# Layer 1 of a two-layer decoder: where the states are added, how the convolution is done, and which banks the scores use

## The chip, the core and the metric

The kernel runs on one core of one Trainium2 chip. A core has five engines that run side by side: TensorE (PE, with its weight loads as PEld) multiplies matrices, VectorE (DVE), ScalarE (ACT) and GpSimd (POOL) work element by element, and SyncE (SP) issues the transfers between memory and the on-chip SBUF. Matmul results land in PSUM, eight banks of 512 f32 per partition. Each engine executes its own instructions in the order in which the program issued them; between engines, semaphores make one wait for another. The metric is the device time of one execution in microseconds.

## The reference

The input is `x`, 64 sequences of 128 tokens with 128 features, with a context of 77 tokens per sequence. Two decoder layers follow one another; each is a mixer, a cross attention with 16 heads over the context, and a feed-forward block, with a residual sum and a layer norm behind each. Layer 0 has a linear attention, a cross attention with an additive bias, and a mixture of ten experts. Layer 1 has a selective scan, a cross attention with a norm of its own, and a feed-forward block with ternary weights. The mixer of layer 1, cut to what matters:

```python
z = x @ W_in + b_in
xc, xr = z[..., :256], silu(z[..., 256:])
xt = causal depthwise convolution of xc over the tokens, 4 taps   # zeros ahead of the first token
xc = silu(xt + conv_b)
dt, Bm, Cm = split(xc @ x_proj_w)                                 # 16 columns each
delta = softplus(dt @ dt_proj_w + dt_bias)
h = exp(delta * A) * h + (delta * xc) * Bm                        # 16 states per channel, step by step over the tokens
y = sum over the 16 states of h * Cm, + xc * D
out = (y * xr) @ W_out + b_out
```

The cross attention of layer 1 computes `softmax(q k / 8) v` with heads of 64; that of layer 0 adds `attn_bias` and a mask to its scores before the softmax.

## The kernel before, in words

Both layers work on groups of four sequences, so that a tile is 128 partitions by 512 columns; there are 16 groups. Layer 0 runs for all groups and leaves its result in memory (`mid`), then layer 1 runs for all groups.

The order of the work is written by a planner, the class `Flow`, when the program is built. Each stage of a group is a generator that yields steps; a step names its engine, a cost in microseconds, its key, the keys that it depends on and the kinds of buffers (slots) that it needs. `Flow.run` keeps up to five groups open and always issues the step that can start first by its own clocks; a group that is further along wins a tie. A buffer can be taken again when the keys in its `until` are done. A ScalarE step that needs another function table ranks 1.3 later. Steps marked `port=True` (those of VectorE and GpSimd that share a way to SBUF) never overlap in the plan. `ahead` moves a step forward in rank. What the planner fixes is the order in which each engine gets its instructions; on the chip the engines wait for data and buffers only.

The mixer of layer 1 in stages:

- `scan_inputs`: loads a group (line 948), transposes it (953, 957), projects it by the first half of `W_in` (`pz`, line 963) into a bank, and ScalarE writes that with the bias into `xp` (line 969), a tile with three zero columns ahead of each sequence. The convolution is four matmuls per half of the channels (line 977), each with a diagonal matrix of one tap (`diag`, line 851) and `xp` shifted by one token. Then silu into `u` (992, 996), the gate from the second half of `W_in` (999, 1008), the projection to dt, B and C (1013) whose rows go to memory (1021), and softplus in pieces (1028 to 1059), the last three of them on GpSimd, ending in `delta` and `du`.
- `spread`: two states make a step. For each step SP fetches the rows of B and of C and spreads them over the partitions, 512 KB each (line 1075), into two buffers each.
- `decays`: ScalarE makes `dA` (line 1090). `states`: VectorE makes `bu = du * B` into PSUM (line 1106) and scans both states (`h`, line 1114). 
- `outputs`: GpSimd multiplies `h` by C in place (line 1138). An order is added by hand: this product starts only after VectorE's `bu` of the next step. TensorE then adds both states into the bank `acc` by matmuls with the identity (line 1151), two matmuls per step, each of which runs as two passes in f32, so four instructions. After eight steps VectorE adds the skip term (1162), and after sixteen come the gate, the output projection (1179), the residual sum (1189) and the norm.

Layer 1's cross attention (`cross_inputs`, `values`, `attend`) makes scores for eight heads at a time (line 1297) in two of five banks, taken one by one: even heads in one, odd heads in the other. VectorE takes the maximum over the context (line 1316, 128x308 elements) and subtracts it (line 1320), once per bank. Exponential, sum, division on GpSimd (1335), transposes (1342), weighted values (1362) and the output projection (1394) follow; the feed-forward block is `feed`.

Layer 0's cross attention (`b_seq`) does the same in two of eight banks (line 586) and adds the bias on VectorE, once per bank (line 603).

Layer 1 has eight PSUM banks: five for general use (`bank`), two for `bu`, one for `acc`.

Of the kernel before, what the change touches and what calls it, by code (L numbers as in the profile page):

```python
# [11 lines left out]
ALU = mybir.AluOpType  # L12
# [25 lines left out]
class Slots(list):  # L38


    def __init__(self, tiles):
        super().__init__(Slot(a) for a in tiles)

# [119 lines left out]
def decoder(ctx: ExitStack, tc: tile.TileContext, t: dict, out: bass.AP):  # L163
# [116 lines left out]
    with (  # L280
# [10 lines left out]
        bank = slots(8, ps, [P, 512], "mm")  # L291
# [215 lines left out]
        def b_load(g):  # L507
# [4 lines left out]
            bias.until = [k + ("sum", b, 1, 1) for b in range(G)]  # L512
# [63 lines left out]
        def b_seq(g, b):  # L576
# [4 lines left out]
            for hf in range(2):  # L581

                def scores(s0, s1, *_):
                    for jj, sc in enumerate((s0, s1)):
                        q4 = slice(32 * (2 * hf + jj), 32 * (2 * hf + jj) + 32)
                        mm(  # L586
                            sc[:, 0 : 4 * M], qT[q4, b * P : (b + 1) * P],
                            kb[q4, b, :, :].rearrange("p h m -> p (h m)"), start=True, stop=True,
                        )

                if hf == 0:
                    *sc, ss, mx = yield PE(0.6, k + ("sc", b, hf), [k + ("qT",), k + ("kb", 3)], scores, bank, bank, sl_s, sl_mx)
# [3 lines left out]
                else:  # L596
                    sc = yield PE(0.6, k + ("sc", b, hf), [], scores, bank, bank)
                for jj in range(2):
                    key = k + ("sum", b, hf, jj)
                    sc[jj].until = key  # L600
                    yield DVE(
                        0.48, key, [k + ("sc", b, hf), k + ("both",)],
                        lambda: dve.tensor_tensor(  # L603
                            s[:, 8 * hf + 4 * jj : 8 * hf + 4 * jj + 4, :],
                            sc[jj].tile[:, 0 : 4 * M].rearrange("p (h m) -> p h m", h=4),
                            bias[:, b, :].unsqueeze(1).to_broadcast([P, 4, M]), ALU.add,
                        ),
                    )
# [228 lines left out]
    with (  # L837
# [10 lines left out]
        diag = new(pc, [P, 2, 4, P], "diag")  # L848
        for c in range(2):
            for k in range(4):  # L850
                dve.tensor_scalar(diag[:, c, k, :], ident, conv_w[:, c, k : k + 1], None, ALU.mult)
# [6 lines left out]
        for c in range(8):  # L858
            bvb = new(p, [P, P], f"xT{c % 2}")
# [15 lines left out]
        pm = new(ps, [P, 3], "mm0")  # L875
# [22 lines left out]
        bank = slots(5, ps, [P, 512], "mm")  # L898
        sl_x = slots(4, p, [P, G, P], "x")
        sl_xT = slots(2, p, [P, W], "xT")  # L900
        sl_xp = slots(2, p, [P, G, P + 3], "xp")
# [33 lines left out]

        for xp in sl_xp:
            pool.memset(xp.tile[:, :, 0:3], 0.0)
# [7 lines left out]
        def scan_inputs(g):  # L945
# [11 lines left out]
            yield ACT(0.6, k + ("xT",), [k + ("pt",)], lambda: nc.scalar.copy(xT.tile, pt.tile))  # L957
            xT.until = k + ("pr", 1)
            pcv = []
            for c in range(2):  # L960
                pz, xp = yield PE(
                    0.95, k + ("pz", c), [k + ("xT",)],
                    lambda z, _: mm(z, W_in[:, c * P : (c + 1) * P], xT.tile, start=True, stop=True), bank, sl_xp,
                )
                pz.until = k + ("xp", c)
                xp.until = k + ("cv", c)
                yield ACT(
                    0.7, k + ("xp", c), [k + ("pz", c)],
                    lambda: act(
                        xp.tile[:, :, 3:], pz.tile.rearrange("p (b s) -> p b s", b=G), AF.Identity,  # L970
                        bias=b_in[:, c : c + 1],
                    ),
                )

                def conv(pv, taps):
                    for i in taps:
                        mm(
                            pv.rearrange("p (b s) -> p b s", b=G), diag[:, c, i, :],
# [655 lines left out]
```

## Time and profile before

| | |
|---|---|
| Time, median of 3 runs | 3838.25 us (3835.81 to 3839.14) |
| The profiled execution's own time | 3840.87 us |
| Its span | 3839.2 us, 55,872 instructions |
| TensorE busy | 3245.0 us (85%) |
| VectorE busy | 2729.6 us (71%) |
| ScalarE busy | 2107.0 us (55%) |
| GpSimd busy | 1448.3 us (38%) |
| GpSimd's products h * C (line 1138) | 256 of 2348 ns |
| TensorE's accumulation (line 1151) | 1024 of 684 ns, busy 565.4 us |
| VectorE's scans (line 1114) | 256 of 2285 ns |
| VectorE's products bu (line 1106) | 256 of 1324 ns |
| Score reductions, subtractions in layer 1 (1316, 1320) | 256 of 465 ns, 256 of 477 ns |
| Score sums in layer 0 (603) | 256 of 468 ns |

The page gives, for one execution, each engine's busy time, the span in forty slices with the busy share of each in tenths, the TensorE clock that was granted in tenths of full speed, and the costliest groups of instructions: line, engine, operation, what is written and read, count, busy time, mean duration, and the idle time of the engine just before them with what ended it. Matmuls overlap one another, so the busy time of a group can be less than count times mean. Answers of the trace add the same for a stretch of the span, the waits (who waited for whom), the chain of work that ended last, and instructions in order of time. Layer 0 ends at about 1508 us in this trace; layer 1's first scan starts at 1571.

### The profile page before, as it was taken

The page shows a single profiled execution, that of the slowest core. Times are in us where ns is not written, and L with a number is a line of the kernel's source. Part 1 is how long each engine was busy: PE and PEld are TensorE (multiplying, and loading weights), DVE is VectorE, ACT ScalarE, POOL GpSimd, SP SyncE. Part 2 cuts the span into 40 slices and gives each one's busy share as a digit, 9 for nine tenths or more (in the row PEclk, how much of TensorE's full clock was granted, in tenths as well). Part 3 has the DMA queues.
Part 4 walks back from the last instruction along what each step waited for, and adds up shares of the span by engine and source line. Part 5 has one row for each costly group of instructions (what it writes and reads, how often), then busy time and mean ns, then how long its engine had stood idle before and what let it go on. Part 6 is the DMA issues. An engine that isn't in the chain of part 4 may idle for free.

```text
span 3839.2 us, 55872 instructions
## 1 busy us (share of the span) xinstructions
PE 3245.0 (85%) x20696; PEld 2080.1 (54%) x20696; DVE 2729.6 (71%) x5399; ACT 2107.0 (55%) x3690; POOL 1448.3 (38%) x1222
## 2 busy tenths in 40 slices
PE   5999999999999998568877978769788978887783
PEld 3676666666666665224643636435544645554462
DVE  5866766666767554577587687786887788778874
ACT  3663555555554422435745757556566657655653
POOL 4321222222222100455345344544445545545531
PEclk8999999999999998789989999879888988988896
DMA  2000000000000001464154151444243435434410
GB/s 84 11 2 22 12 12 12 12 12 12 11 12 12 4 6 53 154 217 168 33 173 152 43 163 62 155 157 126 96 153 125 139 110 169 143 107 140 143 42 6
DMA packets 126134, 312.86 MB, mean 81 GB/s; under 512 B 29714, under 2 KB 51620, under 8 KB 125476
## 3 DMA queue, kind: packets, MB, share of 16 engines
q1 hardware_dynamic: 125860, 309.29, 24.8%
q8 instruction: 162, 2.65, 0.3%
q14 instruction: 112, 0.92, 0.1%
HBM read 299.29 MB, written 9.96 MB: 81 GB/s over the span
## 4 chain that ended last, share of the span: by engine, by line
PE 49%; DVE 21%; POOL 10%; DMA 9%; ACT 5%; issue 4%; SPq 1%; DVEq 0%; POOLq 0%; ACTq 0%
DMA B<-rows 8%; PE mm L770 7%; PE mm L742 7%; PE mm L743 6%; DVE h L1114 5%; POOL h L1138 4%; DVE bu L1106 3%; PE mm L652 3%; PE acc L1151 3%; PE mm L629 3%; PE mm L1342 2%; PE mm L1362 2%; PE mm L586 2%; POOL s L1335 1%; PE mm L1394 1%
## 5 line engine op out<-in xcount | busy, mean ns | idle before, releaser
L1138 POOL TENSOR_TENSOR h<-h,C 128x1024 f32<-128x1024 f32 x256 | 600.6, 2348 | 586.1 <-DVE bu L1106 488.6
L1151 PE MATMUL acc<-h,ident 128*128 128x512 f32 x1024 | 565.4, 684 | 207.1 <-POOL h L1138 184.5
L1114 DVE TENSOR_TENSOR_SCAN h<-dA,bu 128x1024 f32<-128x1024 f32 x256 | 585.1, 2285 | 47.2 <-PE acc L1151 9.7
L1090 ACT ACTIVATE dA<-delta,negA 128x508 f32<-128x508 f32 x512 | 337.7, 711 | 297.5 <-DVE h L1114 292.1
L1106 DVE TENSOR_TENSOR bu<-du,B 128x1024 f32<-128x1024 f32 x256 | 338.9, 1324 | 202.5 <-DMA B<-rows 123.2
L1151 PEld LDWEIGHTS acc<-h,ident 128*128 128x128 f32 x1024 | 199.8, 212 | 473.3 <-POOL h L1138 282.1
L757 ACT ACTIVATE a<-mm 128x512 f32<-128x512 f32 x320 | 187.4, 596 | 328.6 <-PE mm L742 221.1
L770 PEld LDWEIGHTS mm<-w,eh 128*128 128x128 f32 x2560 | 308.6, 193 | 66.1 <-issue 39.4
L742 PE MATMUL mm<-cT,w 128*128 128x512 f32 x640 | 334.8, 605 | 9.5 <-DVE s L603 9.2
L743 PE MATMUL mm<-cT,w 128*128 128x512 f32 x640 | 329.6, 597 | 0.0
L770 PE MATMUL mm<-w,eh 128*128 128x128 f32 x2560 | 315.9, 277 | 11.5 <-DVE eh L760 11.0
L791 DVE SCALAR_TENSOR_TENSOR v<-mm,cw,v 128x128 f32<-128x128 f32 x512 | 143.5, 343 | 217.5 <-PE mm L770 217.2
L760 DVE TENSOR_TENSOR eh<-a,mm 128x512 f32<-128x512 f32 x320 | 214.0, 674 | 58.0 <-ACT a L757 53.5
L612 POOL TENSOR_TENSOR s<-s,mx 128x1232 f32<-128x1232 f32 x64 | 144.3, 2254 | 272.5 <-DVE mx L609 197.9
L1335 POOL TENSOR_TENSOR s<-s,rs 128x1232 f32<-128x1232 f32 x64 | 144.5, 2259 | 217.3 <-DVE rs L1329 183.2
L743 PEld LDWEIGHTS mm<-cT,w 128*128 128x128 f32 x640 | 122.6, 192 | 155.6 <-issue 142.1
L1342 PE MATMUL mm<-ident,s 128*77 128x128 f32 x1024 | 160.3, 310 | 54.9 <-POOL s L1335 46.6
L1297 PEld LDWEIGHTS mm<-kT,qT 64*128 64x128 f32 x2048 | 151.3, 215 | 96.9 <-DVE s L1320 46.5
L1297 PE MATMUL mm<-kT,qT 64*128 64x77 f32 x2048 | 171.5, 309 | 28.3 <-DVE s L1320 27.7
L1342 PEld LDWEIGHTS mm<-ident,s 128*77 128x77 f32 x1024 | 138.4, 171 | 100.9 <-POOL s L1335 64.9
L1353 ACT COPY pT<-mm 77x512 f32<-77x512 f32 x256 | 139.2, 581 | 83.0 <-PE mm L1342 81.1
L1241 PE MATMUL mm<-xT,w_yWq 128*128 128x256 f32 x512 | 161.0, 396 | 15.1 <-ACT kT L1233 9.4
(288 smaller groups left out, 6556.8 us busy)
## 6 DMA issues: line engine op xcount, KB each, us to landing
B<-rows SPq DMA_DIRECT2D x256, 512.0 KB, 4.9
C<-rows SPq DMA_DIRECT2D x256, 512.0 KB, 4.1
cg<-in_ctxT SPq DMA_DIRECT2D x32, 154.0 KB, 2.9
x<-in_x SPq DMA_DIRECT2D x16, 256.0 KB, 3.5
mid<-x SPq DMA_DIRECT2D x16, 256.0 KB, 2.1
xb<-mid SPq DMA_DIRECT2D x16, 256.0 KB, 2.9
x<-mid SPq DMA_DIRECT2D x16, 256.0 KB, 5.4
out<-x SPq DMA_DIRECT2D x16, 256.0 KB, 2.5
```

The lines of the kernel that those rows point to most:

```text
L742: mm(p1, w1[:, e, c * P : (c + 1) * P], xT, start=True, stop=True)
L743: mm(p3, w3[:, e, c * P : (c + 1) * P], xT, start=True, stop=True)
L757: yield ACT(0.6, key + ("silu",), [key], lambda: act(a.tile, p1.tile, AF.Silu), table="silu")
L760: lambda: dve.tensor_tensor(h[:, c, :], a.tile, p3.tile, ALU.mult),
L770: mm(py[:, b * P : (b + 1) * P], hf[:, j % 2, b * P : (b + 1) * P], w2[:, f, j % 2, :], start=j == 0, stop=j == n - 1,)
L1090: act(dA[:, j, :, 1:], delta[:, c, :, 1:], AF.Exp, scale=negA[:, c, n + j : n + j + 1])
L1106: order[g, c, n] = dve.tensor_tensor(bu, du[:, c, :].unsqueeze(1).to_broadcast([P, 2, W]), BC["B", g, c, n], ALU.mult)
L1114: dve.tensor_tensor_scan(h.rearrange("p n s -> p (n s)"), DA[g, c, n].rearrange("p n b s -> p (n b s)"), bu.tile.rearrange("p n s -> p (n ...
L1138: one = pool.tensor_tensor(h, h, BC["C", g, c, n], ALU.mult)
L1151: mm(acc, ident, HS[g, c, n][:, j, :], start=n + j == 0, stop=n + j == NS - 1)
L1297: mm(sc[:, i * M : (i + 1) * M], qT[r, 4 * hf + i, b2 * P : (b2 + 1) * P], kT[r, 4 * hf + i, b2 * M : (b2 + 1) * M], start=True, stop=True,)
L1342: nc.tensor.transpose(pt[0:M, i * P : (i + 1) * P], s[:, 4 * q + i, :], ident)
```

## The change

Three things are changed.

- In layer 1, behind each product `h * C`, GpSimd adds the second state of the step to the first (a new step `pair`, 128x512, marked `port`), and TensorE accumulates one state instead of two: one matmul (two passes) per step. The planner's costs of these steps change with it.
- The convolution's taps are multiplied into the input projection: four weight matrices `taps[k] = W_in[:, 0:256] * conv_w[:, k]` are made once at the start of layer 1, and the convolution is four matmuls from the transposed input itself, whose tile `xT` now has the three zero columns. The projection `pz`, its eviction into `xp` and the `diag` tiles go. The input bias goes into the silu's bias (`conv_all`); at the first three tokens, where taps are missing, a small matmul with three rows (`first` by a piece of the identity, 12 columns) takes the surplus off again. Other readers of `xT` skip the three columns.
- In both layers the scores of a half go into a pair of neighbouring banks, taken together, and VectorE treats both banks in one instruction of 616 elements: in layer 0 the sum with the bias, in layer 1 the maximum and the subtraction. The banks are numbered as four pairs in layer 0, and as two pairs and a single one in layer 1; single users take any half.

```diff
+class Both:
+    def __init__(self, tile_, parts):
+        self.tile, self.parts = tile_, parts
+    @property
+    def until(self):
+        u = [p.until for p in self.parts]
+        if None in u:
+            return None
+        return [key for v in u for key in (v if isinstance(v, list) else [v])]
...
+def banks(pairs, singles):
+    one, two = Slots([]), Slots([])
+    one.extend(Slot(s) for s in singles)
+    for pair in pairs:
+        halves = [Slot(pair[:, i, :]) for i in range(2)]
+        one.extend(halves)
+        two.append(Both(pair, halves))
+    return one, two
...
-        bank = slots(8, ps, [P, 512], "mm")
+        bank, bank2 = banks([new(ps, [P, 2, 512], f"mm{i}") for i in range(4)], [])
...
-                for jj in range(2):
-                    key = k + ("sum", b, hf, jj)
-                    sc[jj].until = key
-                    yield DVE(
-                        0.48, key, [k + ("sc", b, hf), k + ("both",)],
...
+                sc.until = k + ("sum", b, hf)
+                yield DVE(
+                    0.8, k + ("sum", b, hf), [k + ("sc", b, hf), k + ("both",)],
...
-        diag = new(pc, [P, 2, 4, P], "diag")
-        for c in range(2):
-            for k in range(4):
-                dve.tensor_scalar(diag[:, c, k, :], ident, conv_w[:, c, k : k + 1], None, ALU.mult)
+        taps = new(pc, [P, 4, 256], "taps")
+        nc.sync.dma_start(out=taps.rearrange("p k c -> p (k c)"), in_=t["conv_rows"].to_broadcast([P, 1024]))
+        dve.tensor_tensor(taps, taps, W_in[:, 0:256].unsqueeze(1).to_broadcast([P, 4, 256]), ALU.mult)
+        conv_all = new(pc, [P, 2], "conv_all")
+        dve.tensor_reduce(conv_all, conv_w, AX.X, ALU.add)
+        dve.tensor_tensor(conv_all, conv_all, b_in[:, 0:2], ALU.mult)
+        dve.tensor_tensor(conv_all, conv_all, conv_b, ALU.add)
+        first = new(pc, [3, 256], "first")
+        b_first = new(p, [3, 256], "B1")
+        nc.sync.dma_start(out=b_first, in_=rows("b_row", 256, 3))
+        missing = new(p, [3, 3, 256], "B0")
+        pool.memset(missing, 0.0)
+        for k in range(3):
+            nc.sync.dma_start(
+                out=missing[0 : 3 - k, k, :],
+                in_=t["conv_rows"][:, k * 256 : (k + 1) * 256].to_broadcast([3 - k, 256]),
+            )
+        dve.tensor_tensor(first, missing[:, 0, :], missing[:, 1, :], ALU.add)
+        dve.tensor_tensor(first, first, missing[:, 2, :], ALU.add)
+        dve.scalar_tensor_tensor(first, first, -1.0, b_first, ALU.mult, ALU.mult)
...
-        bank = slots(5, ps, [P, 512], "mm")
+        bank, bank2 = banks([new(ps, [P, 2, 512], f"mm{i}") for i in range(2)], [new(ps, [P, 512], "mm2")])
...
-        sl_xT = slots(2, p, [P, W], "xT")
-        sl_xp = slots(2, p, [P, G, P + 3], "xp")
+        sl_xT = slots(2, p, [P, G, P + 3], "xT")
...
-                pz, xp = yield PE(
-                    0.95, k + ("pz", c), [k + ("xT",)],
-                    lambda z, _: mm(z, W_in[:, c * P : (c + 1) * P], xT.tile, start=True, stop=True), bank, sl_xp,
-                )
...
+                def conv(pv, ks):
+                    pv = pv.rearrange("p (b s) -> p b s", b=G)
+                    cs = slice(c * P, (c + 1) * P)
+                    for i in ks:
+                        mm(pv, taps[:, i, cs], xT.tile[:, :, i : i + P], start=i == 0, stop=False)
+                    if 3 in ks:
+                        edge = ident[0:3, 0:3].unsqueeze(1).to_broadcast([3, G, 3])
+                        mm(pv[:, :, 0:3], first[:, cs], edge, start=False, stop=True)
...
-                yield POOL(2.0, ("C", g, c, n), deps, product, ahead=AHEAD, port=True)
+                yield POOL(2.2, ("C", g, c, n), deps, product, ahead=AHEAD, port=True)
+                pair = HS[g, c, n]
+                yield POOL(
+                    1.3, ("pair", g, c, n), [], lambda: pool.tensor_tensor(pair[:, 0], pair[:, 0], pair[:, 1], ALU.add),
+                    ahead=AHEAD, port=True,
+                )
 
                 def add(acc):
-                    for j in range(2):
-                        mm(acc, ident, HS[g, c, n][:, j, :], start=n + j == 0, stop=n + j == NS - 1)
+                    mm(acc, ident, pair[:, 0, :], start=n == 0, stop=n + 2 == NS)
...
-                    *sc, s, mx = yield PE(1.2, k + ("sc", b, hf), [kk + ("k", 7)], scores, bank, bank, sl_s, sl_mx)
+                    sc, s, mx = yield PE(1.2, k + ("sc", b, hf), [kk + ("k", 7)], scores, bank2, sl_s, sl_mx)
...
-                for o in range(2):
-                    sc[o].until = k + ("sub", b, hf, o)
-                    h4 = slice(8 * hf + 4 * o, 8 * hf + 4 * o + 4)
-                    sc4 = sc[o].tile[:, 0 : 4 * M].rearrange("p (i m) -> p i m", i=4)
-                    yield DVE(
-                        0.45, k + ("max", b, hf, o), [k + ("sc", b, hf)],
...
+                sc.until = k + ("sub", b, hf)
+                h8 = slice(8 * hf, 8 * hf + 8)
+                sc8 = sc.tile[:, :, 0 : 4 * M].rearrange("p o (i m) -> p o i m", i=4)
...
+                yield DVE(
+                    0.8, k + ("max", b, hf), [k + ("sc", b, hf)],
+                    lambda: dve.tensor_reduce(by_half(mx.tile), sc8, AX.X, ALU.max),
+                )
```

## The prediction

> **What bounds the kernel now.** I read the slices first, then the busy time by stage, then the waits of the engine that stays fullest, then the shapes that the change touches. The slices split the run in two.
>
> ```profile
> PE   5999999999999998568877978769788978887783
> ...
> DVE  5866766666767554577587687786887788778874
> ...
> POOL 4321222222222100455345344544445545545531
> PEclk8999999999999998789989999879888988988896
> ```
>
> The stages, as stretch, length, then busy time (instructions) of PE, PEld, DVE, ACT, POOL, granted clock, DMA share, GB/s (from two answers):
>
> ```profile
> 0.00:1508.00 1508.00, 1423.06 (x10630) 965.78 (x10630) 997.40 (x2679) 755.88 (x1314) 368.15 (x513) 0.98 0.05 15
> ...
> 2776.00:3575.00 799.00, 665.39 (x3740) 418.25 (x3740) 644.44 (x1009) 505.55 (x889) 403.69 (x264) 0.88 0.41 134
> 3679.00:3839.00 160.00, 92.68 (x748) 69.80 (x747) 84.22 (x252) 74.67 (x148) 36.73 (x46) 0.76 0.02 6
> ...
> 1571.00:3839.00 2268.00, 1781.69 (x9964) 1095.90 (x9964) 1717.78 (x2683) 1322.30 (x2339) 1072.88 (x701) 0.88 0.38 125
> ```
>
> Layer 0 (to 1508) is TensorE's: 94% busy at clock 0.98. Layer 1 (from 1571) is nobody's alone: PE 79%, DVE 76%, ACT 58%, POOL 47%. In the regular part, 2776 to 3575, six groups take 799 us, 133 each, and PE (83%) and DVE (81%) share the lead. So work taken from PE is worth only what DVE waits for PE. Those waits, DVE's own, for the whole of layer 1:
>
> ```profile
> engine line waited for: us in total, times, longest us
> DVE bu L1106 <- DMA B<-rows: 123.2, 113, 4.0
> DVE bu L1106 <- POOL du L1059: 76.3, 12, 8.4
> DVE xb L1401 <- PE mm L1394: 73.3, 18, 10.5
> DVE mx L1316 <- PE mm L1297: 49.1, 35, 7.0
> ...
> DVE x L1534 <- PE mm L1528: 24.0, 12, 2.9
> ```
>
> With three smaller ones (9.7 and 5.3 on acc, 1.4 on L1179) DVE loses 163 us to PE, 76 to POOL and 123 to the landing of B. The shapes:
>
> ```profile
> L1138 POOL TENSOR_TENSOR h<-h,C 128x1024 f32<-128x1024 f32 x256 | 600.6, 2348 | 586.1 <-DVE bu L1106 488.6
> L1151 PE MATMUL acc<-h,ident 128*128 128x512 f32 x1024 | 565.4, 684 | 207.1 <-POOL h L1138 184.5
> ...
> L1106 DVE TENSOR_TENSOR bu<-du,B 128x1024 f32<-128x1024 f32 x256 | 338.9, 1324 | 202.5 <-DMA B<-rows 123.2
> ```
>
> Last, what happens when GpSimd and DVE both read two SBUF operands: the timeline at the start of group 12 (start, length), where a GpSimd add of the size that the change adds begins 0.07 us ahead of DVE's bu product.
>
> ```profile
> 3174.94 1.27 POOL L1217 TENSOR_TENSOR xb<-x,bo_all 128x512 f32<-128x512 f32 x1
> 3175.01 2.29 DVE L1106 TENSOR_TENSOR bu<-du,B 128x1024 f32<-128x1024 f32 x1 [7.46 <-POOL du L1059]
> ```
>
> The bu product takes 2.29 us there and 1.23 alone (its median in the line's own view): it waits for the add to end, then runs. The scan, which reads only one operand from SBUF, keeps its 2.29 us beside any GpSimd product.
>
> **The change part by part.** The sum is made against the profiled execution, 3840.87 us with a span of 3839.2; the median of the timed runs, 3838.25, is 2.6 below it.
>
> Accumulation. 512 of 1024 acc matmul passes go: half of 565.4, -283 us of PE. The first half of the input projection goes too, -36.8 (its 64 passes, line 963), and 64 tiny edge passes come; the nearest rows are the 128-column f32 passes at 0.28 us (line 770), so at most +18. PE in layer 1: 1782 - 283 - 37 + 18 = 1480 us, 65% instead of 79%. By queueing, waits go as load over idle share: 0.79/0.21 = 3.8 to 0.65/0.35 = 1.9, a half of 163, so -82. But the clock speaks against the whole half: the rows give 0.98 at 94% busy, 0.88 at 83%, 0.76 at 58%. A line through the last two gives 0.79 at 65%, with which 1480 us become 1650 (73%, ratio 2.7, waits -47). I take -60, between the two; the ends are 0 and -163.
>
> The page "TensorE: Matmul & The Clock Gate" of the Trainium skill (Part 1) has a harder rule: only half and full clock exist, and an idle window of about 3.4 us drops to half. If the freed PE time fell in such windows, PE would give DVE nothing back, and the sum would be 60 us worse; the 0.88 that a PE busy 79% was granted speaks for the mixture instead.
>
> The pair add. GpSimd gets 256 adds of 128x512. The rows with two tensors of that shape (lines 1411, 1217, 1172, 1417) have means from 1.27 to 1.49, and 1.27 where nothing disturbs; half of the 2.35 product is 1.17. I take 1.27: 325 us, POOL from 1073 to 1398 of 2268 (62%). It still fits, so the add itself costs nothing as long as the next product waits for bu anyway (488.6 us of such idle time now). Two things behind it do cost. First, turns: the product of step i starts when bu of step i+1 ends and takes 2.35, the scan beside it 2.29, so in a run of steps the new add starts just when bu of step i+2 wants to. Over the 224 steps that have a step two behind them in their group, bu starts within 1.27 us after the product's end in about 73; the overlap adds up to 90 us. Ends: 0 (the planner holds the two apart by its shared-port clock and puts reductions between) and 90. I take 30, a third: steps in a run already wait for B (123 us), and part of the delay falls into that. Second, du: the three GpSimd steps before a group's first bu queue behind products, and now adds; one add each in the 12 groups that wait now, 12 x 1.27 = +15 (ends 0 and 41, two adds in 16 groups). The accumulator's matmuls start 1.27 later and take half as long; three h buffers cover it, since a step comes every 6.6 us in the regular part and holds h for about 8; without that cover the scan would wait, as it does for 9.7 us now. B and C are freed by bu and the product, not by the add, so SP's queue is moved only where the product is late, which the 30 hold.
>
> On the same edit the Trainium skill's page "GPSIMD Engine Reference" (sections 4.1 and 8) advises VectorE for elementwise work and names contention with DVE instructions that have two SBUF inputs. Read as every bu paying, it would make the term 325 us, and the change 248 us slower by my other terms; the trace shows the mechanism but also that most bu start when GpSimd is between products.
>
> Convolution. Without pz and its eviction (line 969, 21.9 us of ACT) a group's inputs lose some 2 us of latency. That is worth nothing while the first conv matmul waits for the u buffer, which the output projection two groups earlier frees: for group 12 conv begins at 3032, as that projection ends, while pz began at 2943. Without that cover, 14 groups x 2 = -28. Setup: the eight diag products (1.66) go; a 512 KB broadcast, four small loads and seven short DVE operations come, and five issues of about 0.4 us go ahead of the weights and of the first x on SP's queue. Bounds -3 and +7 (B's landing 4.9 plus the issues 2.0); I take +2. The strided copy into xT has its like in line 969, 0.69 against 0.58, on an ACT that is 58% busy: 0.
>
> Scores in bank pairs. From reductions of 308 and 1232 elements, 465 and 1426 ns, an element costs 1.04 ns, so 616 take 785 instead of 2 x 465, a saving of 145; the subtraction 797 instead of 2 x 477, saving 157. 128 of each: -39 us on DVE, which sits in the lead, so I count all of it (other end 0). Layer 0's sum saves 148 x 128 = 19 us on a DVE that is 66% busy under a PE at 94%: 0. The price: a score needs one of two given pairs rather than any two of five banks, and the trace has no such wait. Its nearest row is PE's wait for score banks (line 1297 on DVE's subtraction), 27.7 us, and 46.5 on the weight loads; ends -20 (both banks come free earlier, at 1.6 us instead of 1.9) and +75. I take +5, near the PE row's lower part, since PE has more air.
>
> Sum: -60 + 30 + 15 + 0 + 2 - 39 + 5 = -47. 3840.9 - 47 = 3794, and less 2.6 for the median: **3791**.
>
> **The rivals.** (1) Much faster: PE and DVE bound the period by turns, and with PE at 92 us of a group's 133 instead of 111 the period follows the fullest engine at the 83% that it has now: DVE's 107, less 2.4 of scores, so 105 / 0.83 = 126, 7 us less over 15 groups, -105: 3733. For it: 480 of the 1791 us of the chain of waits between 1700 and 3500 are PE's. Against it: in the regular part DVE waits mostly for du and B, not for PE. (2) Nothing lands: savings of 99 against other terms of 99, 3838. (3) Slower by turns: in runs of back-to-back steps every bu pays 1.27 for the add in front. Without the turns my sum is -77, so it decides from 77 / 1.27 = 61 steps that pay in full; if a freer PE lets the planner pack scans denser and 120 of 256 pay, that is 152 - 77 = +75: 3913. For it: 67 of the steps now follow within 3.7 us; against it: they wait for B two steps on. (4) Score pairs starve: a single user takes one half of each pair and the scores of the 64 sequences each come 1.2 us late, +75 for the 5 I took: 3861. Against it: five banks are rarely full.
>
> **How the numbers follow.** A measurement here can tell about 0.2% (8 us). Forecast (3755 to 3830) 0.41; rival 1 0.21; rival 2 0.08; rival 3 0.20; rival 4 0.10. Faster 0.62, same 0.08, slower 0.30. The unknown terms alone would reach from 3585 (all good ends) to 4051 (all bad ones); 3690 to 3900 leaves out about a fifth: the lower end of rival 1 and the upper half of rival 3. The likeliest case's own range is 3755 to 3830.
>
> **What would show it.** Acc matmuls 512, busy near 290 to 330; GpSimd adds at 1.27; score reductions 128 at 0.79. bu's mean above 1.32 and DVE's idle time on PE down from 163 toward 100 are my two main terms. Layer 1's granted clock between 0.80 and 0.88. Layer 0's end within 10 us of 1508. I am wrong if bu's mean passes 1.6, if PE waits for DVE at the score matmuls by over 100 us, or if layer 0 moves.

## The result, and the profile after

The changed kernel takes 4219.01 us (median of 4 runs, 4213.41 to 4222.31) against 3838.69 us for the kernel before in the same comparison: ratio 1.0988, 95% interval 1.0969 to 1.1007. It is 380 us slower, and the forecast of 3791 us (range 3690 to 3900) was wrong in sign and by more than the range.

The stages of the changed kernel, in the columns of the stage rows of the prediction (stretch, length, busy time of PE, PEld, DVE, ACT, POOL, clock, DMA share, GB/s):

```profile
0.00:1762.00 1762.00, 1520.08 (x10630) 975.47 (x10630) 1000.45 (x2551) 749.52 (x1304) 368.15 (x513) 0.96 0.05 13
1825.00:4216.00 2391.00, 1713.30 (x9456) 1067.72 (x9456) 1790.14 (x2427) 1288.56 (x2298) 1476.72 (x958) 0.78 0.36 118
```

Two thirds of the loss lie in layer 0, the stage to which the prediction gave nothing: it ends at 1762 instead of 1508 (+254 us). TensorE executes the same 10,630 instructions there, but is busy 86% of the time instead of 94%. Layer 1 takes 2391 us instead of 2268 (+123). From the end of layer 0 to the first scan, with the setup of the taps, it takes 65 us, against 63 before.

The groups that the change touches, from the page after (busy time, mean ns, then the idle time ahead of them and what ended most of it):

```profile
L1178 POOL TENSOR_TENSOR h<-h,C 128x1024 f32<-128x1024 f32 x256 | 607.7, 2374 | 336.0 <-issue 93.4
...
L1195 PE MATMUL acc<-h,ident 128*128 128x512 f32 x512 | 387.3, 850 | 303.8 <-POOL h L1190 276.8
...
L1146 DVE TENSOR_TENSOR bu<-du,B 128x1024 f32<-128x1024 f32 x256 | 398.0, 1555 | 102.2 <-DMA B<-rows 96.2
...
L1190 POOL TENSOR_TENSOR h<-h 128x512 f32<-128x512 f32 x256 | 384.8, 1503 | 19.5
```

Half of the accumulating passes are gone, but a pass takes 850 ns instead of 684. The `bu` products pay 231 ns each more (1324 to 1555), and the new add takes 1503 ns.

VectorE's waits in layer 1 (who waited for whom: total us, times, longest):

```profile
DVE bu L1146 <- DMA B<-rows: 96.2, 66, 8.4
DVE mx L1366 <- PE mm L1347: 88.9, 42, 13.3
DVE fh L1542 <- ACT fh L1538: 56.5, 27, 7.1
DVE h L1154 <- PE acc L1195: 46.2, 28, 6.2
DVE xb L1452 <- PE mm L1445: 36.3, 16, 5.0
```

The wait of `bu` for `du`, 76.3 us before, is nearly gone (3.6); but the maximum over the scores waits longer for TensorE (88.9 against 49.1), and so does the scan for the accumulation (46.2 against 9.7). TensorE does less in layer 1, and VectorE waits for it more: 252 us in all its waits for TensorE there, against 163 before.

### The profile page after: what moved, and what is told of

Its sections match the earlier page's. It is cut to its first block, busy times and chain, and to the rows that moved or that the text cites. A ratio compares the mean times of both kernels' runs of the same rounds, so it can differ in the third digit from the quotient of the medians.

```text
span 4216.8 us, 54152 instructions
## 1 busy us (share of the span) xinstructions
PE 3272.0 (78%) x20184; PEld 2061.2 (49%) x20184; DVE 2805.7 (67%) x5014; ACT 2061.2 (49%) x3632; POOL 1852.6 (44%) x1479
## 4 chain that ended last, share of the span: by engine, by line
PE 46%; DVE 25%; ACT 10%; POOL 8%; DMA 5%; issue 4%; SPq 1%; DVEq 0%; ACTq 0%; POOLq 0%
PE mm L798 6%; DVE h L1154 5%; PE mm L770 5%; PE mm L771 5%; DMA B<-rows 4%; DVE bu L1146 4%; POOL h L1178 3%; PE mm L680 2%; PE mm L1413 2%; PE mm L1393 2%; PE acc L1195 2%; PE mm L657 2%; PE mm L1445 2%; PE mm L1315 2%; PE mm L1347 2%
## 5 line engine op out<-in xcount | busy, mean ns | idle before, releaser
L1154 DVE TENSOR_TENSOR_SCAN h<-dA,bu 128x1024 f32<-128x1024 f32 x256 | 585.5, 2287 | 76.4 <-PE acc L1195 46.2
L1195 PE MATMUL acc<-h,ident 128*128 128x512 f32 x512 | 387.3, 850 | 303.8 <-POOL h L1190 276.8
L1146 DVE TENSOR_TENSOR bu<-du,B 128x1024 f32<-128x1024 f32 x256 | 398.0, 1555 | 102.2 <-DMA B<-rows 96.2
L1190 POOL TENSOR_TENSOR h<-h 128x512 f32<-128x512 f32 x256 | 384.8, 1503 | 19.5
L770 PE MATMUL mm<-cT,w 128*128 128x512 f32 x640 | 348.0, 626 | 44.1 <-DVE v L819 15.4
L798 PE MATMUL mm<-w,eh 128*128 128x128 f32 x2560 | 333.7, 283 | 44.5 <-DVE eh L788 30.5
L771 PE MATMUL mm<-cT,w 128*128 128x512 f32 x640 | 337.7, 610 | 5.2 <-DVE v L819 3.6
L1195 PEld LDWEIGHTS acc<-h,ident 128*128 128x128 f32 x512 | 105.1, 245 | 454.9 <-POOL h L1190 391.4
L1393 PE MATMUL mm<-ident,s 128*77 128x128 f32 x1024 | 181.3, 331 | 82.8 <-POOL s L1386 43.3
L1347 PE MATMUL mm<-kT,qT 64*128 64x77 f32 x2048 | 179.5, 330 | 61.0 <-DVE s L1370 33.5
L1347 PEld LDWEIGHTS mm<-kT,qT 64*128 64x128 f32 x2048 | 160.4, 237 | 134.4 <-DVE s L1370 57.3
L1393 PEld LDWEIGHTS mm<-ident,s 128*77 128x77 f32 x1024 | 150.6, 184 | 139.6 <-POOL s L1386 69.9
L1288 PE MATMUL mm<-xT,w_yWq 128*128 128x256 f32 x512 | 176.6, 428 | 45.8 <-ACT kT L1280 25.6
```

Of the source, the lines that this page charges most:

```text
L770: mm(p1, w1[:, e, c * P : (c + 1) * P], xT, start=True, stop=True)
L771: mm(p3, w3[:, e, c * P : (c + 1) * P], xT, start=True, stop=True)
L798: mm(py[:, b * P : (b + 1) * P], hf[:, j % 2, b * P : (b + 1) * P], w2[:, f, j % 2, :], start=j == 0, stop=j == n - 1,)
L1146: order[g, c, n] = dve.tensor_tensor(bu, du[:, c, :].unsqueeze(1).to_broadcast([P, 2, W]), BC["B", g, c, n], ALU.mult)
L1154: dve.tensor_tensor_scan(h.rearrange("p n s -> p (n s)"), DA[g, c, n].rearrange("p n b s -> p (n b s)"), bu.tile.rearrange("p n s -> p (n ...
L1190: 1.3, ("pair", g, c, n), [], lambda: pool.tensor_tensor(pair[:, 0], pair[:, 0], pair[:, 1], ALU.add),
```

## The experiments: what the bank pairs cost

From this profile I suspected neither the add nor the shortage of banks. Every bank that a single user takes is now a half of a tile of two banks. When the program is built, its dependencies follow tiles, so a matmul that writes one half could be made to wait for the readers of the other half, with which it has nothing to do. The rivals: GpSimd's add (its turns with VectorE), and the taking of scores in pairs.

**Halves without pairs, layer 0.** No score is taken in a pair here; each half is a bank of its own in the plan.

```diff
-        bank = slots(8, ps, [P, 512], "mm")
+        pairs = [new(ps, [P, 2, 512], f"mm{i}") for i in range(4)]
+        bank = Slots([pair[:, i, :] for pair in pairs for i in range(2)])
```

> The kernel before, with layer 0's eight banks made as the halves of four two-bank tiles; every engine keeps its instructions and their order. Theory S (shared tiles: a matmul into one half of a tile waits for the reader of the other half): layer 0 ends near 1700 to 1760 us instead of 1508, and the time is 4030 to 4090. Theory O (order: scores come late because two given banks must be free together, and the planner builds a worse order): the order is the old one, so 3838 within 10.

Measured: 4118.75 us, ratio 1.0747 (1.0716 to 1.0778), some 29 us above the range that the shared tile was given, and far from its rival's. The two programs, laid side by side as built, have the same instructions in the same order on every engine, in the same eight banks. They differ in the waits alone: 621 of TensorE's instructions, some 400 of ScalarE's and 350 of VectorE's wait for a later event or for one more engine. Nearly all of TensorE's changed waits (618 of 625) are for an instruction that uses the other half of the same tile. The trace shows the same stretch of TensorE's work in both kernels (start, length, line, and in brackets the idle time ahead with what ended it). Before:

```profile
668.53 0.38 PE L667 MATMUL mm<-w_xWo,oT 128*128 128x128 f32 x2
668.75 0.81 PE L398 MATMUL mm<-w_w_qkv,T 128*128 128x384 f32 x2
669.40 1.02 PE L742 MATMUL mm<-cT,w 128*128 128x512 f32 x2
...
673.54 1.91 PE L629 MATMUL mm<-ident,s 128*77 128x128 f32 x16
675.29 0.81 PE L398 MATMUL mm<-w_w_qkv,T 128*128 128x384 f32 x2
```

With halves:

```profile
781.94 0.38 PE L668 MATMUL mm<-w_xWo,oT 128*128 128x128 f32 x2
782.16 0.81 PE L399 MATMUL mm<-w_w_qkv,T 128*128 128x384 f32 x2
783.93 1.13 PE L743 MATMUL mm<-cT,w 128*128 128x512 f32 x2 [0.96 <-DVE eh L761]
...
788.43 1.91 PE L630 MATMUL mm<-ident,s 128*77 128x128 f32 x16
791.20 0.88 PE L399 MATMUL mm<-w_w_qkv,T 128*128 128x384 f32 x2 [0.86 <-ACT pT L621]
```

The same matmuls take 6.76 us from the first to the last start before, and 9.26 us here: an expert's projection (line 743) first waits for VectorE's `eh` of an earlier one, and later the projection of line 399 waits for ScalarE's copy of `pT`. These waits are short and many, so the list of waits hardly shows them. The idle time between TensorE's expert matmuls (line 770 before, 771 here) tells more, first before, then with halves:

```profile
L770 PE MATMUL mm<-w,eh 128*128 128x128 f32 x2560 | 315.9, 277 | 11.5 <-DVE eh L760 11.0
```

```profile
L771 PE MATMUL mm<-w,eh 128*128 128x128 f32 x2560 | 330.7, 281 | 54.9 <-DVE eh L761 41.4 <-ACT kb L553 3.6 <-DVE y L466 3.3
```

**The same in layer 1**, with four of its five banks as halves.

```diff
...
-        bank = slots(5, ps, [P, 512], "mm")
+        pairs = [new(ps, [P, 2, 512], f"mm{i}") for i in range(2)]
+        bank = Slots([new(ps, [P, 512], "mm2")] + [pair[:, i, :] for pair in pairs for i in range(2)])
```

> The kernel before, with four of layer 1's five banks made as the halves of two two-bank tiles; order unchanged. Theory S: layer 1 grows by 60 to 130 us, the time is 3900 to 3970. Theory O, and theory T (GpSimd's adds and VectorE's bu products take turns, and that is layer 1's loss): 3838 within 10.

Measured: 4000.59 us, ratio 1.0427 (1.0405 to 1.0448), again above the range of the theory that it bears out. The order is that of before, and some 440 of TensorE's instructions have a later or an additional wait, all of them for an instruction that uses the other half of the same tile. So shared tiles alone cost 166 us in layer 1, although TensorE is busy only 79% of the time there.

**The change with layer 0's scores and banks as before.**

```diff
-        bank, bank2 = banks([new(ps, [P, 2, 512], f"mm{i}") for i in range(4)], [])
+        bank = slots(8, ps, [P, 512], "mm")
...
-                    (sc,) = yield PE(0.6, k + ("sc", b, hf), [], scores, bank2)
+                    sc = yield PE(0.6, k + ("sc", b, hf), [], scores, bank, bank)
...
```

> The changed kernel with layer 0's scores and banks put back. Layer 0 should end at 1508 again and layer 1 keep its 123 us: 3965, between 3950 and 3980.

Measured: 3972.13 us (median of 2 runs), ratio 1.0358 (1.033 to 1.0386), inside the range. Layer 0 ends at 1510. So layer 0's pairs are worth 0.063 of the time, 242 us of the 380.

**The change with single banks in both layers**; the add and the convolution remain. Layer 0's edits are those just shown, layer 1's are of the same kind.

```diff
...
-        bank, bank2 = banks([new(ps, [P, 2, 512], f"mm{i}") for i in range(2)], [new(ps, [P, 512], "mm2")])
+        bank = slots(5, ps, [P, 512], "mm")
...
```

> The changed kernel with the scores of both layers put back to two single banks each, so that the GpSimd add and the new convolution stay. Theory S for the whole loss: the prediction's remaining terms, -60 + 30 + 15 + 2 = -13, so 3826, between 3780 and 3850. Theory T: layer 0 is healed and layer 1 keeps its 123 us, so 3960.

Measured: 3883.11 us, ratio 1.0125 (1.0102 to 1.0147), between the values of the two theories (3826 and 3960). Layer 1's pairs thus cost 0.023, some 89 us net: less than the 166 us of the halves alone. The merged reductions are the likely difference, but the order of the work differs too. And without any pair the kernel is still slower than before: the rest of the sum was wrong as well.

**Pairs that nobody shares, layer 0.** The kernel before, with layer 0's scores in one pair of banks of their own, merged sums, and six single banks for everything else.

```diff
-        bank = slots(8, ps, [P, 512], "mm")
+        bank = slots(6, ps, [P, 512], "mm")
+        bank2 = Slots([new(ps, [P, 2, 512], "sc0")])
...
```

> The kernel before with layer 0's scores in one pair of banks of their own, one VectorE instruction per pair, and the other six banks single tiles. Theory S: nobody shares a tile, so layer 0 ends within 20 us of 1508 and the time is 3825 to 3860 (two banks fewer for the rest). Theory O (a pair is scarce): with a single pair it is scarcer than in the changed kernel, so layer 0 grows by more than 100 us.

Measured: 3868.5 us, ratio 1.0092 (1.0069 to 1.0115), with layer 0's end at 1548. That is above both bounds of theory S (3860, and 20 us from 1508), and far from the 100 us and more of theory O. Merged scores with nothing shared cost about 40 us in that layer, not 250: the pair as such, two banks fewer for the rest, and the new order together are a small part of it. A gain of the merged sums isn't to be seen in this stage, whose bound is TensorE. The same was not tried in layer 1.

## The experiments: what the add costs, and what the relief brings

**The add alone**, on the kernel before, with the planner's costs of the change.

```diff
-                yield POOL(2.0, ("C", g, c, n), deps, product, ahead=AHEAD, port=True)
+                yield POOL(2.2, ("C", g, c, n), deps, product, ahead=AHEAD, port=True)
+                pair = HS[g, c, n]
+                yield POOL(
+                    1.3, ("pair", g, c, n), [], lambda: pool.tensor_tensor(pair[:, 0], pair[:, 0], pair[:, 1], ALU.add),
+                    ahead=AHEAD, port=True,
+                )
...
-                    for j in range(2):
-                        mm(acc, ident, HS[g, c, n][:, j, :], start=n + j == 0, stop=n + j == NS - 1)
+                    mm(acc, ident, pair[:, 0, :], start=n == 0, stop=n + 2 == NS)
...
-                    (acc,) = yield PE(1.9, ("acc", g, c, n), [("C", g, c, n)], add, sl_acc)
+                    (acc,) = yield PE(0.86, ("acc", g, c, n), [("pair", g, c, n)], add, sl_acc)
...
```

> The kernel before with the GpSimd add of a step's two states alone. Theory S: -55 + 30 + 15 = -10, so 3828, between 3790 and 3860. Theory T: 3930 to 3960, with bu's mean at 1.5 us or more and the adds' mean above 1.4.

Measured: 3878.66 us, ratio 1.0108 (1.0081 to 1.0135): slower by a good 1%, and between the two theories. `bu` has a mean of 1594 ns and the add one of 1535.

**Relief without the add.** TensorE accumulates only the first state, and GpSimd adds nothing.

```diff
-                    for j in range(2):
-                        mm(acc, ident, HS[g, c, n][:, j, :], start=n + j == 0, stop=n + j == NS - 1)
+                    mm(acc, ident, HS[g, c, n][:, 0, :], start=n == 0, stop=n + 2 == NS)
...
-                    (acc,) = yield PE(1.9, ("acc", g, c, n), [("C", g, c, n)], add, sl_acc)
+                    (acc,) = yield PE(0.86, ("acc", g, c, n), [("C", g, c, n)], add, sl_acc)
...
```

> The kernel before, with TensorE accumulating only the first state of each step and no add on GpSimd (the second state's part of the sum is left out). It has the relief of TensorE without the adds. If the relief is worth what the prediction took for it, 55 to 60 us, this is 3780; the single add's run stands at +44, so the adds would then cost about 100, in line with the 127 us by which VectorE's own instructions grew there. If TensorE's relief is worth nothing because VectorE is the fuller engine, 3830 to 3845, and the adds cost about 45.

Measured: 3912.88 us, ratio 1.0209 (1.0186 to 1.0232): with 512 passes fewer the kernel is slower, which none of the values foresaw. Two suspects were left: the planner's cost of 0.86, which moves the order of everything in layer 1, and the clock, which falls in that layer from 0.88 to 0.79. The next two kernels tell them apart.

**The same relief in the order of before**: half_acc with the planner's cost left at 1.9.

```diff
-                    (acc,) = yield PE(0.86, ("acc", g, c, n), [("C", g, c, n)], add, sl_acc)
+                    (acc,) = yield PE(1.9, ("acc", g, c, n), [("C", g, c, n)], add, sl_acc)
...
```

> The kernel before, except that TensorE accumulates only the first state of a step (what the second state gives to the output is left out; GpSimd adds nothing), and unlike in half_acc the planner's cost of that step stays 1.9, so that every engine keeps the order of before. 512 of the 1,024 accumulating passes go, some 280 us of TensorE's busy time at the clock of before. Theory R (order): half_acc was slower because the changed cost made the planner order all of layer 1 anew; with the old order the relief shows: 3,780 to 3,825 us, ratio 0.985 to 0.997. Theory K (clock): the freed time lowers the granted clock (0.79 in half_acc against 0.88) and the remaining matmuls use it up, whatever the order: 3,834 us and above, with layer 1's clock below 0.83 and passes of 0.8 us.

Measured: 3805.18 us, ratio 0.9916 (0.9896 to 0.9936), inside the range of theory R. The clock of layer 1 falls to 0.81 and the remaining passes take 800 ns, as theory K had it, and yet the kernel gains:

```profile
L1150 PE MATMUL acc<-h,ident 128*128 128x512 f32 x512 | 360.4, 800 | 260.9 <-POOL h L1138 239.0 <-DVE u L1161 20.8 <-DVE s L1319 1.1
```

**The order alone**: the kernel before, all its work in place, with only the planner's cost at 0.86.

```diff
-                    (acc,) = yield PE(1.9, ("acc", g, c, n), [("C", g, c, n)], add, sl_acc)
+                    (acc,) = yield PE(0.86, ("acc", g, c, n), [("C", g, c, n)], add, sl_acc)
...
```

> The kernel before with the same work, where only the planner's cost of an accumulating step is 0.86 instead of 1.9, as the change has it. Theory R (order): the new order of layer 1 alone costs some 2 per cent, 3,880 to 3,930 us, ratio 1.012 to 1.025, with TensorE's share and its clock in layer 1 as before or a little below. Theory K (clock): the order is worth little, 3,820 to 3,850 us, ratio 0.997 to 1.004.

Measured: 3926.32 us, ratio 1.0234 (1.0212 to 1.0255), as R has it. A number that no instruction carries costs 91 us.

**The add in the order of before**: issued in the product's own step, costs 2.0 and 1.9 as before.

```diff
                         tc.add_manual_dep(one.ins, order[behind].ins.name, BEHIND, reason="shared reads")
+                    pool.tensor_tensor(h[:, 0], h[:, 0], h[:, 1], ALU.add)
...
-                    for j in range(2):
-                        mm(acc, ident, HS[g, c, n][:, j, :], start=n + j == 0, stop=n + j == NS - 1)
+                    mm(acc, ident, HS[g, c, n][:, 0, :], start=n == 0, stop=n + 2 == NS)
```

> The kernel before with GpSimd's add of the two states issued straight behind the product in the product's own step, and the planner's costs of before (2.0 for GpSimd's step, 1.9 for TensorE's), so that the order of every engine is that of before. Against half_same it has the add alone on top. Theory T (turns): VectorE's time grows by 100 to 130 us as in add_only (bu at 1.55 to 1.65 us) and the step of GpSimd by 1.5 us; ratio 0.02 to 0.04 above that of half_same. Theory R (order): most of the 1.1 per cent of add_only came from the planner's new order, so this kernel lies at 0.99 to 1.003, and only some 40 us above half_same.

Measured: 3913.87 us, ratio 1.0197 (1.0175 to 1.0219). Against the same kernel without the add (3805.18) it is 109 us, 0.028 of the time before: theory T, except that VectorE grows a little less than it said. R is wrong here: in this order the add has a cost of its own. With the planner's new costs, and the add as a step of its own, the same work takes 35 us less (3878.66 against 3913.87). The price holds for the order of before alone: with the cost 0.86 the kernel with the add (1.0108) is faster than the one without (1.0209), but the planner orders those two differently. The stages of layer 1 carry it; first the relief alone, then relief and add:

```profile
1571.00:3806.00 2235.00, 1637.75 (x9452) 1028.41 (x9452) 1720.89 (x2683) 1323.13 (x2341) 1072.00 (x702) 0.81 0.38 127
```

```profile
1571.00:3919.00 2348.00, 1655.07 (x9452) 1033.04 (x9452) 1815.06 (x2685) 1328.38 (x2346) 1473.38 (x959) 0.81 0.36 121
```

VectorE's busy time grows by 94 us of the 109 (1720.89 to 1815.06), though its instructions are the same. GpSimd is at 63%, so it is not full. The groups of `bu` and of the add in the second kernel, and `bu` in the first:

```profile
L1106 DVE TENSOR_TENSOR bu<-du,B 128x1024 f32<-128x1024 f32 x256 | 421.9, 1648 | 183.0 <-DMA B<-rows 106.2 <-POOL du L1059 74.2 <-DVE xb L1401 0.2
L1143 POOL TENSOR_TENSOR h<-h 128x512 f32<-128x512 f32 x256 | 380.9, 1488 | 20.1
```

```profile
L1106 DVE TENSOR_TENSOR bu<-du,B 128x1024 f32<-128x1024 f32 x256 | 341.0, 1332 | 187.6 <-DMA B<-rows 107.7 <-POOL du L1059 75.6 <-DVE xb L1400 0.2
```

`bu` takes 81 us more. How, the timeline of the kernel with the add shows (start, length):

```profile
2990.41 1.27 POOL L1143 TENSOR_TENSOR h<-h 128x512 f32<-128x512 f32 x1
2990.93 1.84 DVE L1106 TENSOR_TENSOR bu<-du,B 128x1024 f32<-128x1024 f32 x1 [1.45 <-DMA B<-rows]
...
3004.24 2.35 POOL L1138 TENSOR_TENSOR h<-h,C 128x1024 f32<-128x1024 f32 x1
...
3005.60 2.09 DVE L1106 TENSOR_TENSOR bu<-du,B 128x1024 f32<-128x1024 f32 x1 [0.56 <-DMA B<-rows]
...
3006.67 2.13 POOL L1143 TENSOR_TENSOR h<-h 128x512 f32<-128x512 f32 x1
```

A `bu` that starts 0.52 us into an add waits 0.75 us for its end and is done 1.09 us after that. The second `bu` starts during a product and is done 1.10 us after its end, and the add that starts while this `bu` runs is stretched in turn (2.13). Over the whole run, 92 of the 256 `bu` start while GpSimd is idle and take 1.23 us in the mean; 113 start during an add and take 1.88, which makes 73 us; 35 start during a product and take 1.82, which makes 21 us, against 8 without the add. The wait does not go into the wait for B, as I had hoped: `bu` waits 106.2 us for B with the add and 107.7 without, and pays its turn on top.

**The planner's cost at the measured duration.** Since a wrong number cost 91 us, would the right one gain? A step of two passes takes about 1.4 us.

```diff
-                    (acc,) = yield PE(1.9, ("acc", g, c, n), [("C", g, c, n)], add, sl_acc)
+                    (acc,) = yield PE(1.4, ("acc", g, c, n), [("C", g, c, n)], add, sl_acc)
...
```

> The kernel before with the same work, where the planner's cost of an accumulating step is 1.4, its measured duration (two passes of 0.684 us), instead of 1.9. Theory R as 'an honest cost gives a better order': at or below before, 3,800 to 3,838 us, ratio 0.990 to 1.001. Theory R as 'any other order than the one of before costs': 3,850 to 3,930 us, ratio 1.004 to 1.024.

Measured: 3855.24 us, ratio 1.0057 (1.0036 to 1.0078). This is in the range of the second reading, that any other order costs. The honest cost is not the best one; 1.9 gives the better order of the three that were run. Why that order is better stays open. The same 500 us of layer 1, for the kernel before, half_same, cost_only and add_same in this order:

```profile
2900.00:3400.00 500.00, 420.52 (x2343) 263.19 (x2342) 401.68 (x613) 323.04 (x576) 254.88 (x166) 0.89 0.42 140
```

```profile
2900.00:3400.00 500.00, 391.53 (x2315) 253.28 (x2310) 421.50 (x656) 325.92 (x574) 254.47 (x163) 0.86 0.41 138
```

```profile
2900.00:3400.00 500.00, 382.49 (x1909) 222.60 (x1907) 373.44 (x527) 274.45 (x486) 238.71 (x148) 0.86 0.40 133
```

```profile
2900.00:3400.00 500.00, 386.81 (x2303) 248.96 (x2302) 413.01 (x641) 313.90 (x553) 343.73 (x222) 0.86 0.39 131
```

In the new order (third) every engine does less in the same stretch: no engine is the bound, all of them wait more.

**The convolution alone**, on the kernel before: taps in the projection, everything else as it was.

```diff
-                        mm(
-                            pv.rearrange("p (b s) -> p b s", b=G), diag[:, c, i, :],
-                            xp.tile[:, :, i : i + P], start=i == 0, stop=i == 3,
-                        )
...
+                        mm(pv, taps[:, i, cs], xT.tile[:, :, i : i + P], start=i == 0, stop=False)
...
```

> The kernel before with the taps multiplied into the input projection alone. The prediction's terms: +2 for the setup, 0 to -30 for the latency, and a few us for TensorE's 37 less: 3825 to 3842. If the conv stands on the path of a group's inputs: 3800 to 3815.

Measured: 3851.62 us, ratio 1.0048 (1.0034 to 1.0062), some 18 us slower and above both expectations. TensorE's and ScalarE's work fell as planned: 64 passes of the projection go (36.8 us), 64 small ones come (12.4 us busy), and so do ScalarE's 32 evictions (21.9 us). But steps that go change the plan, as a cost does: VectorE's scaling `fh<-fh,q` (128x512, one source in SBUF) goes from 502 to 759 ns, 16.5 us in all, and the accumulating passes from 684 to 708. Whether that is the whole cause wasn't told apart from the order as such. Next to the add (1.0125 against 1.0108) the convolution can't be told from nothing.

Of the kernels that do all of the work none is faster than the one before.

## Why the prediction was wrong

In units of the time before, the change of +0.099 is made of 0.063 for layer 0's pairs, 0.023 for layer 1's, about 0.002 (not told from nothing) for the convolution, and 0.011 for the add with its relief. These are differences of kernels whose planned orders differ too, so each holds that as well. Step by step:

- **"Scores in bank pairs ... I take +5"** is the step that decided. It asked how often a pair is free, looked for the price at PE's wait for score banks, and so found ends of -20 and +75. The price was in the `banks` function: every single user got half of a shared tile, and with it false dependencies. Halves alone cost 284 us in layer 0 and 166 in layer 1. That layer 0 counted 0 in the sum was the same error: a stage with TensorE at 94% has no air for later waits, of which the run with the halves had 621. Rival 4 had the right place, and its condition named the halves of a pair, but it priced 75 us at 64 sequences in layer 1. Of the three signs of being wrong only "if layer 0 moves" came true: `bu`'s mean stayed below 1.6 (1.555), and at the score matmuls TensorE waits for VectorE only 33.5 us in layer 1 (for the subtraction) and 17.9 in layer 0 (for the sum). The halves runs, in which no score is paired, show that the price falls on every user of the banks.
- **"-39 us on DVE"**, the merged score instructions: the sizes were right, 784 and 791 ns measured (785 and 797 forecast). The gain is not visible beside what sharing costs.
- **Turns, "I take 30, a third", and du, +15**: the mechanism was right, the size was not. In the order of before the add costs 109 us against 45 for both terms, inside the sum of their ends (0 to 131). `bu` pays 81 us. More of them start within an add than the 73 that I had counted (113), and each loses 0.65 us. So the end of 90 was the better value, and the third that I took of it was a hope: the delay did not fall into the wait for B. VectorE's one-source scaling `fh<-fh,q` takes turns too (494 to 659 ns, 10.6 us), which I had not counted. The du term is nothing: 75.6 us of waits without the add, 74.2 with it.
- **"I take 1.27" for the add** holds where nothing disturbs; the mean is 1488 to 1535 ns, since GpSimd also waits for its turn.
- **"I take -60" for TensorE's relief**: it brings 31 us in the order of before, inside its ends, but not by the road described. TensorE's busy time in layer 1 falls from 1782 to 1638 us where 283 us of passes go, as the clock falls from 0.88 to 0.81: the forecast of 1650 at 0.79, which had the convolution's 19 us less in it, was close for this kernel, while the changed kernel has 1713 at 0.78. The clock records of these traces hold 0.5 and 1.0 alone, so that 0.88 is a mean over time; the relief is neither nothing, as the prediction had it for freed time that all falls into half clock, nor 60. VectorE's waits for TensorE hardly move (`xb` 73.3 to 75.2, `mx` 49.1 to 48.9). What falls is `bu`'s wait for B (123.2 to 107.7) and small ones. The rule that waits go as load over idle share has no support here.
- **The planner's costs** were no term of the sum at all. They are part of the diff, and in the runs they are worth from -35 us (with the add, which is a step of its own there) to +108 us (half_acc against half_same), as much as any of the engines' terms.
- **The convolution, 0,** was +18 us alone, outside its ends of -28 to 0, and nothing measurable beside the add. The setup, +2, can't be told: from the end of layer 0 to the first scan it is 63 us before, 65 in the changed kernel, 62 in the one without any pairs and 60 in the one with the convolution alone.

Of the rivals, (3), slower by turns, had the mechanism of a good part of what is left without the pairs (1.0125, 3883 us against its 3913). That the times are close is partly luck, since the relief was smaller than its sum had it and the planner's costs were not in it. On this row the Trainium skill's page "GPSIMD Engine Reference" (section 8), which warns of contention with VectorE where an instruction has two SBUF inputs or uses a two-port mode, agrees with the runs in kind for `bu` (1332 to 1648 ns). The skill's page "VectorE: DVE Perf Modes" (section "Mode 2×_2P — use both read ports for one tensor") would explain the one-source scaling (494 to 659 ns): by that section such an operation may read its tensor through both ports. No run here shows the mode itself. The price per collision is the measured one: the rest of the other's instruction, and not every time; here 148 of the 256 `bu` start during an add or a product.

## What to carry to other kernels

A buffer that is cut out of a larger tile brings the larger tile's dependencies along: before merging two operations by means of a common tile, ask who else uses its parts, and compare the waits of the built programs, not only the instructions. An elementwise operation moved to GpSimd beside VectorE operations with two SBUF inputs is to be charged with the turns that they take, at the far end of the bound unless a row shows the cover. Where a planner orders the work, a changed cost is a change of its own, of 0.6 to 3% here: measure each change once in the old order, or the order will be taken for its effect.

## What was not expected of the hardware

- A one-source f32 operation of VectorE in SBUF takes turns with GpSimd too: `fh<-fh,q` (128x512) goes from 494 to 659 ns with the add. There 43 of the 64 start while GpSimd is idle and take 474 ns; 11 start during a GpSimd instruction on two 128x512 tensors and take 851 to 1497. The scan (2285 ns) and the score reductions from PSUM (465 ns) keep their durations (2285 and 466).
- Freed time of TensorE is partly taken back by its clock: with half of the accumulating passes gone, the rest of them takes 800 ns instead of 684, and the other matmuls of layer 1 some 60 us more, so of 283 us of freed passes 144 stay free. The mean granted clock is 0.81 at 73% busy and 0.88 at 79%. A pass that starts at full clock takes 613 ns before and 623 with the relief, one that starts at half clock 1053 and 1095; what changes is the share at half clock, 166 of 1024 before and 192 of 512 with the relief.
- Yet the clock was not what made half_acc slow: half_same has nearly the same clock (0.81 against 0.79) and is 108 us faster.
